# Two pre-activation attention layers on one core: sums held behind additions, weight differences on another engine, other banks for the last projection and the first statistics

## The chip, the cores and the metric

The kernel runs on one core of a Trainium2 chip. The metric is the device time of one execution in microseconds (us). Five engines work side by side, each through its own queue in order: PE (TensorE, matrix products), DVE (VectorE), ACT (ScalarE), POOL (GpSimd) and SP (SyncE), which here issues most of the transfers. Waits between engines go through semaphores. PE writes its results to PSUM, a small memory of eight banks[...].

## The reference, cut to what matters

Eight images of 32 x 32 tokens with 512 channels, in fp32, go through two layers. Each layer norms its input in 32 groups of channels, makes an attention over the 1024 tokens of an image and adds the result to its input.

```python
x = x + _L0_conv_ref(_gn(x), L0_conv_w_qkv, L0_conv_w_proj, L0_conv_b_proj)
x = x + _L1_conv_ref(_gn(x), L1_conv_Wq, L1_conv_Wk, L1_conv_Wv, L1_conv_Wo, L1_conv_pos_emb_w, L1_conv_pos_emb_h)
...
qkv = xt @ w_qkv                                    # layer 0: 16 heads of 32
attn = jax.nn.softmax(jnp.einsum('bhid,bhjd->bhij', q * SCALE, k), axis=-1)
out = jnp.einsum('bhij,bhjd->bhid', attn, v)        # then tokens x channels
out = out @ w_proj + b_proj
...
scores = attn_q @ k + pos.reshape(B, heads, L, L)   # layer 1: 4 heads of 128
attn = jax.nn.softmax(scores, axis=-1)
out = (attn @ v) @ Wo
```

## The kernel before, in words

**Layout.** Activations are kept transposed, channels on the 128 partitions and tokens along the row, in "blocks" of 128 x 4 x 1024 numbers. Every product of a block with a 512 x 512 weight is made in seven products of quarters instead of eight (`seven`, L397). Four sums of quarters of the activation go in as its "forms" (`forming`, L339, the additions at L360), and four differences of weight quarters (`add_up`, L140, the subtractions at L152) are made once and stored to DRAM; `stream` fetches quarters (`w_p`, `w_o`, `w_qkv` in the profile) on SP in the order of a list, `plan`. A block has two units `u`, and for each of them `seven` runs products into the banks `x`, `y` and `z`, in the order x0, y5, x1, y4, z6, y2, z3. After y5, DVE adds `a` = y + p1 (L411), after y4 `b` = y + p1 (L419); y4 cannot start before `a` is made from the same bank, and y2 not before `b`. ACT copies x to p1 and z to p7. The results leave through a sink: `Plain` for queries, keys and values, `Onto` for a projection with its residual, whose `gather` on POOL (L502) and `add` on DVE (L507, L509) put every part onto the block.

**Projections.** `WP` is the projection of layer 0, `WO` that of layer 1. `after_0` (L891) takes an attention output, makes its forms and runs WP onto the residual `x1T`, with the statistics of the next norm (L259) after each unit. `after_1` (L930) does the same with WO onto `x2T`; `put_out` (L941) transposes results on DVE (L947) and sends them off (L952). For the last image, `after_last` (L968) makes the two products of each unit that need no forms first (`two_first`, L437), then the forms, then the other five (`five_last`, L448).

**Norm.** `group_norm` (L265) is a chain of small DVE operations (`turned` L285 to `var` L296), one POOL operation (`rstd`, L300), and four DVE operations that scale the block (L304). `norm_1` (L905) runs it for the second layer; `second` (L910) begins with the forms of the normed block.

**First attention** (`attention_0`, L590). A step is four heads by 512 queries by 128 keys. `front` makes the scores in a PSUM tile `ps` of four banks, of which there is one (L603), and ACT takes the exponential into `e`, of which there are two (L611). `back` multiplies `e` with the values into the bank `acc` (L622) and DVE adds `e` to a running sum `es` (first two at L631, then L633). After eight steps `finish` sums `es` over the partitions on PE (L643), `normalise` (L560) turns that into reciprocals on DVE (L566 to L584), and POOL multiplies (L588).

**Order.** The loop at L1072 goes through images b = 0 to 8. While PE works on the first attention of image b, `side_by_side` (L995) puts between its steps, by their cost, everything of other images: WP of b-1, WO of b-2 woven with the norm of b-1 (`woven`, L983: from step `start` on, one step of the side work in every `gap`, at the `places` given), the projections and second attention of b-1, and the load, norm and projections of b+1. A scheduler then fixes the order on each engine; `tc.issue_after(x)` makes it place an instruction behind x on its engine. At b = 0 there is no earlier image: there the weights WP, WQ1, WK1, WV1 and WO are fetched and their differences made on POOL (`other_sums`, L1060), beside `before_0` of image 1. At b = 1, `other_keys` takes the place of WO.

**Start.** `load_first` (L811) brings image 0 in, turns it on PE (L830) into banks, of which the first half's four are one tile, copies them with ACT (L837), keeps PE busy with six matmuls whose result is not used (`idle`, L841), and takes the statistics from the copies.

Of the kernel before, what the change touches and what calls it, by code (L numbers as in the profile page):

```python
# [9 lines left out]
F32 = mybir.dt.float32  # L10
# [7 lines left out]
P = 128  # L18
# [9 lines left out]
def quick_path(  # L28
# [98 lines left out]
    class Matrix:  # L127
# [12 lines left out]
        def add_up(self, engines, store, keep=False):  # L140

            t = self.t
            whole = t[:, : CC // 2, :].rearrange("p a (b n) -> p (a b) n", n=NB)
            sums = t[:, CC // 2 :, :].rearrange("p a (b c n) -> p (a b) c n", c=HC, n=HN)
            b11, b12, b21, b22 = [quarter(whole, i) for i in (11, 12, 21, 22)]
            for i, (x, y) in enumerate(
                [(b12, b11), (b22, sums[:, 0]), (b22, b12), (b21, sums[:, 1])]
            ):

                engine = engines[i]  # L150
                with tc.issue_after(last_form[0].ins) if engine is nc.vector else nullcontext():
                    engine.tensor_tensor(sums[:, i], x, y, op=ALU.subtract)  # L152
            d = dram.tile([P, 4, HC, HN], F32, tag="sums", name=f"ws_{self.name}", bufs=8)
            store.dma_start(d, sums)
            self.t = d
            self.kept = (whole, sums) if keep else None
# [163 lines left out]

    added = [None]
# [75 lines left out]
    def seven(fs, u, rows, sink, name, hook=None):  # L397

        product = taken(fs, u, rows)
        x = bank(f"x_{name}")
        product(x, 0, True)
        p1 = snapshot("e1", f"p1_{name}")
        nc.scalar.copy(p1, x)
        yield HC
        y = bank(f"y_{name}")
        product(y, 5, True)
        a = snapshot("es1", f"a_{name}")  # L410
        begun[0] = nc.vector.tensor_add(a, y, p1)  # L411
        sink.early(p1, a)
        yield HC
        product(x, 1, False)
        sink.c11(x)
        yield HC
        product(y, 4, False)
        b = snapshot("es1", f"b_{name}")
        half_done[0] = nc.vector.tensor_add(b, y, p1)  # L419
        sink.middle(b)  # L420
        yield HC
        z = bank(f"z_{name}")
        product(z, 6, True)
        p7 = snapshot("e1", f"p7_{name}")
        nc.scalar.copy(p7, z)  # L425
        yield HC
        product(y, 2, False)
        sink.c12(y, p1)
        if hook is not None:
            hook()  # L430
        yield HC
        product(z, 3, False)
        sink.c21(z, a)
        sink.c22(b, p7)
        yield HC

    def two_first(fs, u, sink, name):  # L437

        product = taken(fs, u, False)
        x = bank(f"x_{name}")  # L440
        product(x, 0, True)
        p1 = snapshot("e1", f"p1_{name}")
        nc.scalar.copy(p1, x)
        product(x, 1, False)
        sink.c11(x)
        return p1

    def five_last(fs, u, sink, name, p1):  # L448
        product = taken(fs, u, False)
        y = bank(f"y_{name}")  # L450
        product(y, 5, True)
        a = snapshot("es1", f"a_{name}")
        nc.vector.tensor_add(a, y, p1)
        sink.early(p1, a)
        product(y, 4, False)
        b = snapshot("es1", f"b_{name}")
        nc.vector.tensor_add(b, y, p1)
        sink.middle(b)
        z = bank(f"z_{name}")
        product(z, 6, True)  # L460
        p7 = snapshot("e1", f"p7_{name}")
        nc.scalar.copy(p7, z)
        product(y, 2, False)
        sink.c12(y, p1)
        product(z, 3, False)
        sink.c21(z, a)
        sink.c22(b, p7)

# [121 lines left out]
    def attention_0(q, k, v, b, blocks=range(NT)):  # L590
# [23 lines left out]
        def back(m, h, j, e):  # L614
# [14 lines left out]
            if j == blocks[1]:  # L629
                state["esum"] = mem.tile([P, HB, NB], F32, tag="es0", name=f"es_{name}", bufs=1)  # L630
                nc.vector.tensor_add(state["esum"], state["first"], e)  # L631
            elif j != blocks[0]:
                nc.vector.tensor_add(state["esum"], state["esum"], e)  # L633
# [153 lines left out]
    def load(b, st):  # L787
# [21 lines left out]
        st["xn"] = yield from forming(x, f"xn0_{b}", behind=lambda: added[0])  # L809

    def load_first(st):  # L811
# [8 lines left out]
        xT = chunks(x)  # L820
        for h in range(NH):
# [13 lines left out]
            for cc in (0, 2, 1, 3):  # L835
                part = xT[cc][:, h * NB : (h + 1) * NB]
                nc.scalar.copy(part, banks[cc])  # L837

# [3 lines left out]
        for cc in (0, 2, 1, 3):  # L842
            statistics(st, xT, cc, "0_0")
# [47 lines left out]
    def after_0(b, st, hook=None):  # L891

        fs = st.pop("ao0") if "ao0" in st else forms(st["q0"], f"ao0_{b}", block(f"forms_{b}"))
        x = st["x1"] = block(f"x1T_{b}")
        xT = fetch(st["kept"], x)
        for u in range(2):
            bias = [bproj_sb[:, n * HC + u : n * HC + u + 1] for n in range(2)]
            stream.unit(WP, False, u)
            yield from seven(
                fs, u, False, Onto(halves(xT, u), bias), f"wp_{b}_{u}", hook if u else None  # L900
            )
            for n in range(2):
                statistics(st, xT, n * HC + u, f"1_{b}")

    def norm_1(b, st, after=None, behind=None):  # L905
        xT = chunks(st["x1"])
        st["kept"] = put_away(xT, f"1_{b}")
        yield from group_norm(st, xT, f"1_{b}", after, behind)

    def second(b, st):  # L910

        fs = forms(st.pop("x1"), f"xn1_{b}")
# [55 lines left out]
    def after_last(b, st):  # L968
# [4 lines left out]
        early = [x[:, :HC, :NB], x[:, HC:, :NB]]  # L973
        p1s = []
        for u in range(2):
            stream.unit(WO, False, u)
            p1s.append(two_first(early, u, sinks[u], f"wo_{b}_{u}"))
        fs = forms(x, f"ao1_{b}")
        for u in range(2):
            stream.unit(WO, False, u)  # L980
            five_last(fs, u, sinks[u], f"wo_{b}_{u}", p1s[u])
# [32 lines left out]

    def marked():
        in_place[0] = True
        return
        yield
# [14 lines left out]

    FIRST = units(WQ0) + units(WK0) + units(WV0, True)
    plan = [(m, m is WV0, u, ORDER) for u in range(2) for m in (WV0, WQ0, WK0)]
    for b in range(B + 1):
        if b >= 1:
            plan += units(WP)
# [8 lines left out]
    plan += [(WO, False, u, some) for some in (FIRST_TWO, LAST_FIVE) for u in range(2)]  # L1047
# [12 lines left out]
    def other_sums():  # L1060
        for m in (WP, WQ1, WK1, WV1, WO):
            m.fetch(nc.gpsimd)
            m.add_up([nc.gpsimd] * 4, nc.gpsimd)
# [8 lines left out]
    for b in range(B + 1):  # L1072
# [11 lines left out]
        if last is not None:  # L1084
            if past is not None:
                norm = norm_1(b - 1, last, after=lambda: half_done[0])
            else:
                norm = norm_1(b - 1, last, behind=lambda: begun[0])
            rest.append(after_0(b - 1, last, forms_past if past is not None else None))
            total += PRODUCT  # L1090
            if past is not None:
                rest.append(woven(later(after_1, b - 2, past), norm, 3, 3))
                total += PRODUCT
            else:
                rest.append(chain(woven(other_keys(b, here), norm, 0, 1), marked()))
# [19 lines left out]
        else:  # L1115
            rest.append(woven(rest_of_first(here), incoming, 0, 2))
            total += PRODUCT
        if coming is not None:

            before = later(before_0, b + 1, coming, forms_0 if last is not None else None)  # L1120
            rest.append(before if last is not None else woven(before, other_sums(), 2, 7))
# [500 lines left out]
```

## Time and profile before

| what | value |
|---|---|
| median of three runs | 3847.89 us (3846.76 to 3849.78) |
| profiled execution, its time | 3848.35 us |
| its span, first to last instruction | 3846.6 us |
| mean granted clock of PE | 0.998 |
| PE busy | 3789.4 us, 99% |
| DVE busy | 2555.1 us, 66% |
| ACT busy | 1760.2 us, 46% |
| POOL busy | 621.6 us, 16% |
| data moved | 234.72 MB, mean 61 GB/s |
| exponentials L611 | 512 of 1878 ns |
| sums L633 | 384 of 2330 ns |
| multiplications L588 on POOL | 128 of 1662 ns |

Lines of the page and of the trace give an engine, the line of the kernel, the operation with the names of its result and its operands, and times in microseconds. A timeline row has its start and its busy time first, then "xN" for how many instructions stand in it, and in brackets the idle time of the engine just before, with the instruction that ended it. In the list of waits, an entry such as "PE ps L603 <- ACT e L611" is the idle time of PE ahead of the scores, ended by an exponential: total, number, longest.

### The profile page before, as it was taken

The numbers are of one execution on the slowest core, as the hardware profiler recorded it, in microseconds if no ns is written. First come the engines' busy times: TensorE is split into PE (matmuls) and PEld (weight loads), VectorE is DVE, ScalarE is ACT, GpSimd is POOL, SyncE is SP. The second block draws the span as 40 slices with busy tenths as digits, with TensorE's granted clock in tenths as the row PEclk, the third lists the DMA queues.
The fourth block names the chain that finished last, engine by engine and source line by source line (L and its number), as shares of the span: only waits on it lengthen the run. The fifth ranks groups of instructions, "written<-read, shape, count | busy, mean of one in ns | idle before, by whom it ended". The sixth has DMA issues, their size and how long they took to land.

```text
span 3846.6 us, 79883 instructions
## 1 busy us (share of the span) xinstructions
PE 3789.4 (99%) x34478; PEld 1376.3 (36%) x34478; DVE 2555.1 (66%) x2966; ACT 1760.2 (46%) x1830; POOL 621.6 (16%) x398
## 2 busy tenths in 40 slices
PE   9999999999999999999999999999999999999998
PEld 4222244222443234432343323433234332334353
DVE  6777775686755866558665686656866568665544
ACT  3554544545444454444544445444454445553132
POOL 1342101121011211012101121111210112001201
PEclk9999999999999999999999999999999999999999
DMA  6122120142202322023120241103311023110321
GB/s 185 61 88 81 41 59 6 44 122 62 56 9 83 89 54 56 13 92 85 45 55 16 93 93 38 50 21 98 90 40 41 26 96 78 33 37 31 109 41 26
DMA packets 482983, 234.72 MB, mean 61 GB/s; under 512 B 269600, under 2 KB 461376, under 8 KB 481600
## 3 DMA queue, kind: packets, MB, share of 16 engines
q1 hardware_dynamic: 470992, 213.74, 20.5%
q0 software_dynamic: 2608, 13.70, 1.0%
q8 instruction: 273, 4.47, 0.5%
q10 hardware_dynamic: 9024, 2.10, 0.3%
q14 instruction: 86, 0.70, 0.1%
HBM read 170.72 MB, written 58.72 MB: 60 GB/s over the span
## 4 chain that ended last, share of the span: by engine, by line
PE 88%; DVE 7%; ACT 2%; issue 2%; DMA 0%; SPq 0%; POOL 0%; DVEq 0%; ACTq 0%; POOLq 0%
PE ps L603 12%; PE ps L718 11%; PE acc L730 11%; PE acc L622 11%; PE y_q L327 4%; PE y_v L327 4%; PE y_k L327 4%; PE ps L719 3%; PE x_q L327 3%; PE x_v L327 3%; PE z_k L327 3%; PE x_k L327 3%; PE z_q L327 3%; PE z_v L327 3%; DVE es L633 2%; ACT e L611 2%
## 5 line engine op out<-in xcount | busy, mean ns | idle before, releaser
L611 ACT ACTIVATE e<-ps 128x2048 f32<-128x2048 f32 x512 | 961.7, 1878 | 840.1 <-PE ps L603 630.0
L633 DVE TENSOR_TENSOR es<-es,e 128x2048 f32<-128x2048 f32 x384 | 894.8, 2330 | 403.7 <-ACT e L611 400.4
L603 PE MATMUL ps<-q,k 32*64 32x512 f32 x8192 | 579.1, 614 | 17.1 <-ACT e L611 17.1
L622 PE MATMUL acc<-e,v 128*32 128x512 f32 x4096 | 546.7, 605 | 0.0
L721 ACT ACTIVATE e<-ps 128x512 f32<-128x512 f32 x512 | 305.7, 597 | 507.1 <-PE ps L719 436.4
L718 PE MATMUL ps<-q,k 128*128 128x512 f32 x1024 | 525.0, 594 | 0.2 <-DVE posT L704 0.2
L730 PE MATMUL acc<-e,v 128*128 128x512 f32 x1024 | 522.0, 593 | 0.3 <-ACT e L721 0.3
L588 POOL TENSOR_TENSOR q<-q,su 128x512 f32<-128x512 f32 x128 | 212.7, 1662 | 1550.3 <-DVE su L584 1427.7
L741 DVE TENSOR_TENSOR es<-es,e 128x512 f32<-128x512 f32 x384 | 290.4, 756 | 251.0 <-ACT e L721 248.4
L719 PE MATMUL ps<-posT,sel 128*128 128x512 f32 x512 | 406.6, 794 | 0.0
L718 PEld LDWEIGHTS ps<-q,k 128*128 128x128 f32 x1024 | 192.5, 190 | 230.1 <-issue 218.5
L603 PEld LDWEIGHTS ps<-q,k 32*64 32x64 f32 x8192 | 120.6, 130 | 410.1 <-issue 223.5
L730 PEld LDWEIGHTS acc<-e,v 128*128 128x128 f32 x1024 | 193.1, 189 | 147.3 <-issue 92.6
L622 PEld LDWEIGHTS acc<-e,v 128*32 128x32 f32 x4096 | 81.3, 108 | 412.7 <-issue 366.1
L631 DVE TENSOR_TENSOR es<-e,e 128x2048 f32<-128x2048 f32 x64 | 171.6, 2681 | 32.8 <-ACT e L611 32.7
L568 DVE STREAM_TRANSPOSE tu<-su 128x512 f32<-128x512 f32 x128 | 90.5, 707 | 97.3 <-ACT su L566 95.7
L719 PEld LDWEIGHTS ps<-posT,sel 128*128 128x128 f32 x512 | 97.3, 190 | 122.5 <-issue 122.5
L566 ACT COPY su<-sums 128x512 f32<-128x512 f32 x128 | 74.9, 585 | 131.2 <-PE sums L643 81.5
L704 DVE TENSOR_TENSOR posT<-pp,posT 32x512 fp32r<-32x512 f32 x128 | 112.0, 875 | 31.9 <-ACT posT L699 30.6
L492 POOL TENSOR_TENSOR k<-b_k,p_k 128x512 f32<-128x512 f32 x32 | 52.0, 1624 | 483.4 <-ACT p_k L425 472.7
L699 ACT CAST posT<-pp 32x512 fp32r<-32x512 f32 x128 | 105.9, 827 | 45.8 <-PE pp L686 44.7
L492 POOL TENSOR_TENSOR v<-b_v,p_v 128x512 f32<-128x512 f32 x32 | 51.6, 1614 | 433.9 <-ACT p_v L425 433.9
(214 smaller groups left out, 4546.0 us busy)
## 6 DMA issues: line engine op xcount, KB each, us to landing
w_qkv<-ws_qkv SPq DMA_DIRECT2D x168, 128.0 KB, 2.5
d<-x0T SPq DMA_DIRECT2D x32, 512.0 KB, 3.0
x1T<-d SPq DMA_DIRECT2D x32, 512.0 KB, 5.9
d<-x1T SPq DMA_DIRECT2D x32, 512.0 KB, 3.6
x2T<-d SPq DMA_DIRECT2D x32, 512.0 KB, 6.1
w_qkv<-in_L_conv_w_qkv SPq DMA_DIRECT2D x126, 128.0 KB, 2.2
out<-ot SPq DMA_DIRECT2D x240, 64.0 KB, 2.0
xs<-in_x SPq DMA_DIRECT2D x224, 64.0 KB, 2.5
```

The lines of the kernel that those rows point to most:

```text
L327: ins = nc.tensor.matmul(out[columns, :], weights[:, columns], moving, start=start, stop=stop, skip_group_check=open_sum,)
L588: nc.gpsimd.tensor_tensor(dst, dst, su, op=ALU.mult)
L603: nc.tensor.matmul(ps[some, r, :], k[m][rows, j * P + 64 * i : j * P + 64 * i + 64], q[m][rows, h * NB : (h + 1) * NB], start=True, stop=True,
L611: nc.scalar.activation(e, ps, AF.Exp, scale=D0 ** -0.5)
L622: nc.tensor.matmul(acc[r * D0 : (r + 1) * D0, :], v[:, j, c0 : c0 + D0], e[:, r, :], start=(j == blocks[0]), stop=(j == blocks[-1]),)
L631: nc.vector.tensor_add(state["esum"], state["first"], e)
L633: nc.vector.tensor_add(state["esum"], state["esum"], e)
L718: nc.tensor.matmul(ps, k[h][:, keys], q[:, h, queries], start=True, stop=False)
L719: nc.tensor.matmul(ps, sel_flat[:, keys], posT[:, h, queries], start=False, stop=True)
L721: nc.scalar.activation(e, ps, AF.Exp, scale=1.0 / math.sqrt(D1))
L730: nc.tensor.matmul(acc, v[:, j, h * D1 : (h + 1) * D1], e, start=(j == 0), stop=(j == NT - 1),)
L741: added[0] = nc.vector.tensor_add(state["esum"], state["esum"], e)
```

## The change

It has five parts.

1. Around every norm of the second layer (WO woven with `norm_1` for b of 2 and more, and the first WP at b = 1), each sum `es` of the first attention is placed behind the last addition `a` or `b` (`reader`). The scalings of the norm (L304) and the forms of the normed block are placed behind sums (`summed`); the norm is taken up at steps 0, 2, 4, 8, 9 and 10 of every 14 instead of every third, with its forms behind it instead of at the head of `second`. At b = 1 the places are 0, 1, 2, 4, 5 and 6 of every 7.
2. At b = 0 the twenty weight differences of WP, WQ1, WK1, WV1 and WO are made on DVE instead of POOL, one by one, each behind a sum of the first attention. The load of image 1 is woven at every step instead of every second.
3. The first WP (image 0) is done in the way of the last WO: the two products of each unit that need no forms first, the forms between them, then the other five. For image 7 the statistics of the second unit are placed behind an addition `a`.
4. In the last WO, unit 1 takes its banks from the attention's PSUM: `x` in `acc`, `y` and `z` in a tile of four banks like `ps`. The forms are interleaved with the first products.
5. In `load_first`, the statistics (bn_stats) read the PSUM banks, each behind ACT's copy of the same bank, and are aggregated after the `idle` matmuls are issued.

The diff, cut to its core:

```diff
+        def adding(self, engines, store, behind, keep=False):
...
-                with tc.issue_after(last_form[0].ins) if engine is nc.vector else nullcontext():
+                with tc.issue_after(behind().ins) if engine is nc.vector else nullcontext():
                     engine.tensor_tensor(sums[:, i], x, y, op=ALU.subtract)
+                yield 0
...
+    reader = [None]
+    summed = [None]
+    beside_norm = [False]
...
-        begun[0] = nc.vector.tensor_add(a, y, p1)
+        reader[0] = begun[0] = nc.vector.tensor_add(a, y, p1)
...
-        half_done[0] = nc.vector.tensor_add(b, y, p1)
+        reader[0] = half_done[0] = nc.vector.tensor_add(b, y, p1)
...
+    def in_two_parts(x, m, sinks, name, room=None, done=lambda u: None, behind=None, banks=(bank, bank)):
+
+        early = [x[:, :HC, :NB], x[:, HC:, :NB]]
+        p1s, fs = [], []
+
+        def products():
+            for u in range(2):
+                stream.unit(m, False, u)
+                p1s.append((yield from two_first(early, u, sinks[u], f"{name}_{u}", banks[u])))
+
+        def sums():
+            fs.extend((yield from forming(x, name, room, behind)))
+
+        yield from woven(products(), sums(), 0, 1)
+        for u in range(2):
+            stream.unit(m, False, u)
+            yield from five_last(fs, u, sinks[u], f"{name}_{u}", p1s[u], banks[u])
+            done(u)
...
-                nc.vector.tensor_add(state["esum"], state["first"], e)
+                other = state["first"]
             elif j != blocks[0]:
-                nc.vector.tensor_add(state["esum"], state["esum"], e)
+                other = state["esum"]
+            if j != blocks[0]:
+
+                with tc.issue_after(reader[0].ins) if beside_norm[0] else nullcontext():
+                    summed[0] = nc.vector.tensor_add(state["esum"], other, e)
...
+        looks = small.tile([P, CC, NH, 6], F32, tag="looks", name="looks")
...
                 nc.scalar.copy(part, banks[cc])
+                nc.vector.bn_stats(looks[:, cc, h, :], banks[cc])
...
-        for cc in (0, 2, 1, 3):
-            statistics(st, xT, cc, "0_0")
+        for cc in range(CC):
+            nc.vector.bn_aggr(
+                st["mv"][:, : 2 * CC].rearrange("p (s c) -> p c s", c=CC)[:, cc, :],
+                looks[:, cc].rearrange("p h s -> p (h s)"),
+            )
...
+        if "ao0" not in st:
+            yield from in_two_parts(
+                st["q0"], WP, sinks, f"wp_{b}", block(f"forms_{b}"), done, lambda: summed[0]
+            )
+            return
...
+    def sums_1(b, st):
+
+        st["xn1"] = yield from forming(st.pop("x1"), f"xn1_{b}", behind=lambda: summed[0])
...
+        idle = [psum.tile([P, NB], F32, tag="acc", name="wo_acc", bufs=1)]
+        scores = psum.tile([P, HB, NB], F32, tag="ps", name="wo_ps", bufs=1)
+        idle += [scores[:, r, :] for r in range(HB)]
+        run(in_two_parts(x, WO, sinks, f"wo_{b}", banks=(bank, lambda name: idle.pop(0))))
...
-            m.add_up([nc.gpsimd] * 4, nc.gpsimd)
+            yield from m.adding([nc.vector] * 4, nc.gpsimd, lambda: summed[0])
...
-                norm = norm_1(b - 1, last, after=lambda: half_done[0])
+                norm = norm_1(
+                    b - 1, last, after=lambda: half_done[0], behind=lambda: summed[0]
+                )
...
+            norm = chain(norm, later(sums_1, b - 1, last))
...
-                rest.append(woven(later(after_1, b - 2, past), norm, 3, 3))
+                rest.append(with_norm(woven(later(after_1, b - 2, past), norm, 3, 14, (0, 2, 4, 8, 9, 10))))
...
-                rest.append(chain(woven(other_keys(b, here), norm, 0, 1), marked()))
+                rest.append(chain(woven(other_keys(b, here), norm, 0, 7, (0, 1, 2, 4, 5, 6)), marked()))
```

## The prediction

> **What bounds the kernel now.** I read the page's busy times first, then the chain that ended last, then the list of what TensorE (PE) waited for, and last the timeline around each of those waits. The page says that PE is busy for 3789.4 us of a span of 3846.6 us, and the chain runs through PE for 88% of it:
>
> ```profile
> PE 3789.4 (99%) x34478; PEld 1376.3 (36%) x34478; DVE 2555.1 (66%) x2966; ACT 1760.2 (46%) x1830; POOL 621.6 (16%) x398
> ...
> PE 88%; DVE 7%; ACT 2%; issue 2%; DMA 0%; SPq 0%; POOL 0%; DVEq 0%; ACTq 0%; POOLq 0%
> ```
>
> The change keeps PE's matmuls, so only the other 57.2 us (3846.6 - 3789.4) can be won. PE's waits (total, times, longest) say where they lie:
>
> ```profile
> PE ps L603 <- ACT e L611: 17.1, 16, 2.9
> PE y_wo L327 <- DVE a_wo L411: 9.1, 6, 1.8
> ...
> PE x_v L327 <- issue: 3.5, 1, 3.5
> PE sums L643 <- DVE es L633: 3.1, 2, 1.8
> PE y_wp L327 <- DVE forms L360: 2.5, 1, 2.5
> ```
>
> In five images, 471 us apart, the same two waits return. The timeline of one (start, duration, engine, line, operation; in brackets the idle time before and its releaser):
>
> ```profile
> 1314.33 2.98 DVE L304 TENSOR_SCALAR x1T<-x1T,back,rstd 128x1024 f32<-128x1024 f32 x4 [1.20 <-POOL rstd L300]
> ...
> 1317.23 2.28 DVE L633 TENSOR_TENSOR es<-es,e 128x2048 f32<-128x2048 f32 x1
> ...
> 1319.60 1.88 ACT L611 ACTIVATE e<-ps 128x2048 f32<-128x2048 f32 x1 [5.25 <-DVE es L633]
> ...
> 1321.54 1.12 PE L603 MATMUL ps<-q,k 32*64 32x512 f32 x16 [0.98 <-ACT e L611]
> ```
>
> Four scalings of the norm stand ahead of a sum `es`; the exponential needs the buffer that this sum frees; PE needs the exponential to empty its scores. The second wait, 9 us on: two sums hold back `a_wo`, which frees the bank of the next product.
>
> ```profile
> 1325.24 4.64 DVE L633 TENSOR_TENSOR es<-es,e 128x2048 f32<-128x2048 f32 x2
> ...
> 1329.80 0.68 DVE L411 TENSOR_TENSOR a_wo<-y_wo,p_wo 128x512 f32<-128x512 f32 x1
> ...
> 1330.54 1.92 PE L327 MATMUL y_wo<-f_ao,w_o 128*32 128x512 f32 x16 [1.42 <-DVE a_wo L411]
> ```
>
> In the first attention GpSimd (POOL) makes the weight differences while DVE makes the sums:
>
> ```profile
> 156.08 9.38 DVE L633 TENSOR_TENSOR es<-es,e 128x2048 f32<-128x2048 f32 x2
> ...
> 156.23 3.76 POOL L152 TENSOR_TENSOR prep_q<-prep_q 128x512 f32<-128x512 f32 x3
> ...
> 165.60 1.07 PE L643 MATMUL sums<-es,ones 128*32 128x512 f32 x8 [1.82 <-DVE es L633]
> ```
>
> Two sums took 9.38 us; elsewhere one takes 2.28.
>
> **What the Trainium skill says.** "SBUF — State Buffer", Who interferes with whom: a DVE instruction with two SBUF inputs contends with a GpSimd instruction that reads SBUF. The trace agrees: 4.69 us for a sum beside L152 against 2.28 alone, and 2.4 to 3.3 us for a POOL subtraction against 1.27. "PSUM — Partial Sum Buffer", PSUM bank collisions: two engines may not touch one bank and quadrant at once, reads by ScalarE and VectorE included, so such reads must be ordered. Parts 4 and 5 put several banks into one tile, and in the changed instruction list they are ordered for the whole tile; no row of before has it. "TensorE: Matmul & The Clock Gate", Part 1: an idle array falls to half its clock and needs some 3.4 us of work to recover. The first `x_v` product agrees: 32 records in 3.46 us, where the next takes about 1.73.
>
> **Part 1, the norms.** In the changed order each sum stands behind the last a or b addition, and the scalings are split in pairs with a sum ahead. Working it with before's times: sum 3 of the row starts at about 1313.0, inside the 1.20 us in which DVE waited for `rstd`, and ends at 1315.3 instead of 1319.5. Its exponential then waits only for its scores, which end at about 1317.85: 1.75 us earlier than 1319.60, more than the 0.98 us of PE's wait. `a_wo` of the second unit moves ahead of its sum and ends at about 1327.3; PE reaches that product at 1329.1 less the 0.98 already won, so the 1.42 goes too. What is late next: `a_wo` of the first unit ahead of sum 1 makes exponential 2 end 0.65 later, 0.3 us before PE's scores need it, and sum 2 has 1.6 us. Nothing else on DVE is behind by more. So 0.98 + 1.42 = 2.4 us an image, 12.0 for five (bounds 5 and 13.5: one wait left, or the slow matmuls after each wait won too). The sixth norm (waits of 1.19 at 3186.99 and 1.31 at 3214.35) is reordered alike: I take 1.5 of 2.5. In the last one `a_wo` is moved ahead of the statistics, and its 1.62 us wait goes: 1.6. The second image's scalings keep their order, so the 1.85 us wait at 376.34 stays.
>
> **Part 2, twenty subtractions to DVE.** 20 x 0.62 us (L152 on DVE at 26.52: five in 3.09) is 12.4 us of DVE, set in gaps of 0.9 to 1.9 us in front of its sums; in exchange each sum beside them falls from about 4.6 to 2.3 us. The last sum then no longer keeps PE waiting at 165.60 (1.82), and the 16 score matmuls after it, slow by 1.82 - 1.11 = 0.71, run at full clock: 2.5. At 137.7 there is a wait of 2.9, but `k`'s addition stands next and would make the following product wait some 1.8, so 0.5 there; 1.0 for five smaller ones. Sum 4.0 (bounds 1 and 7). The first subtraction of each matrix now waits on DVE for its fetch, with sums behind it. Fetches landed 5.7 to 8.0 us after issue on POOL's queue; the first is issued at 135.8 and read at about 156, the others are issued two sums or more ahead, so I count nothing; a fetch late by 3 us would cost that once. The stores wait for DVE on POOL's queue, with a multiplication (L588) behind; POOL was idle for 10 to 20 us there.
>
> **Part 3, first WP.** The 3.5 us of `x` products of the second unit move ahead of `y_wp`, whose forms were late by 2.50 us; the 1.04 us wait ahead of it and the slow product (2.94 against 1.92) go with it: 4.5 (bounds 2 and 5.5). The fetch of `x1T` on SP moves ahead of a weight fetch; it took 5.9 us to land and is needed later than that. POOL's gather now stands before the L588 that the forms need; if `x1T` were late, the forms would be too.
>
> **Part 4, last WO.** `y`, then `z` and `y` of unit 1 lie in one tile. In the changed list the second `y` waits for `a_wo`, `z` for `b_wo`, the next `y` for `z`'s copy, the last `z` for an addition of `y`. Each is 0.59 to 0.69 us and about 0.25 of handing over, four in a row, 3.6 us; before, where a product stood between, these cost 1.1. So +2.5 (bounds 0 and 3.6).
>
> **Part 5, first statistics.** `bn_stats` (0.64) and ACT's copy (0.51) now alternate on the four banks of one tile, and statistics end at about 16.9 instead of 15.6: xn +1.25. The `idle` matmuls (5.32) wait for the last look and run until 22 to 23.5 us, ahead of `x_v`, which then runs warm (1.7 less). But `y_v` now stands ahead of the second `x_v` and needs the second form (25.6), and the following `y_v` needs `a_v`, behind five L152 on DVE (31.8; before 30.27). `b_v` stands behind five more (35.5; before 33.27), and less of the next product is done ahead. I get the first `y_q` ending at 42.3 against 39.1: +3.2 (bounds 0 and 5).
>
> **Sum.** -12.0 - 1.5 - 1.6 - 4.0 - 4.5 + 2.5 + 3.2 = -17.9 us. The profiled execution took 3848.35 us (span 3846.60 and 1.75 around it), 0.46 above the median of 3847.89. So 3830.4 there, and 3830.0 as a median. A difference of 0.2% (7.7 us) is about what a measurement can tell from none.
>
> **Rivals.**
> - Everything is won (0.12): 2.7 in each norm with the slow matmuls, 2.6 and 1.8 in the two others with theirs, 5.5 and 6 in parts 3 and 2, and start and end cost 1 each: -13.5 - 4.4 - 11.5 + 2 = -27.4, 3820.5. For it: the waits stand in the trace. Against it: the tile-wide orders.
> - The waits partly shift (0.18): only 0.98 goes in each norm (4.9), 1.6 in the last, 2.5 and 2 in parts 3 and 2, while start and end cost 4.5 and 3.5: -3.0, 3845. For it: only 0.3 us of slack behind the first `a_wo`.
> - Slower (0.10): the additions that now stand ahead of every sum make all exponentials late. An addition costs 0.65; what goes beyond the 0.3 us of slack, 0.35, falls on each of about seven held sums in seven places: +17.2. With no gain in the norms and the rest at -1.6 - 4.0 - 4.5 + 5.7 = -4.4, this is +12.8, 3861. It decides from the point where PE's score matmuls wait in every round beside a norm. Against it: in before PE has one wait there in nine rounds, and sum 2 has 1.6 us.
> - That the change doesn't do what it says is excluded by the order of instructions.
>
> **How the numbers follow.** My forecast holds 0.60, with its own range 3823 to 3838. Faster by over 0.2% means below 3840.2: 0.60 + 0.12 + 0.05 of the shifted case = 0.77. Within 0.2%: 0.13. Slower: 0.10. The range 3818 to 3845 leaves out the slower case, half of the shifted one at most, and the extreme of the best.
>
> **What would show it.** In the profile after: no wait of a `y_wo` product for `a_wo` (L411 of before) and none of the scores for the exponential in the five norms, the L304 rows split x2; sums near 2.3 us at 141 to 271; no wait of `y_wp` for forms; the first `y_q` some 3 us later; four waits of 0.9 in the last 12 us. I am wrong if PE's waits for exponentials grow in number, or if start and end lose more than 10 us together.

## The result, and the profile after

The changed kernel takes 3858.48 us (median of 13 runs, 3855.73 to 3861.51), the kernel before 3847.74 us (13 runs). The ratio is 1.0026, with a 95% interval of 1.0019 to 1.0033: slower by 10.7 us. The forecast was 3830.0, its range 3818 to 3845. The profiled execution has a span of 3857.9 us. Its busy times, and what PE waited for (total, times, longest):

```profile
PE 3793.1 (98%) x34478; PEld 1370.3 (36%) x34478; DVE 2573.5 (67%) x2986; ACT 1762.0 (46%) x1830; POOL 613.4 (16%) x378
```

```profile
PE ps L637 <- ACT e L645: 25.6, 22, 4.2
PE idle L883 <- DVE looks L879: 5.5, 1, 5.5
...
PE y_wp L335 <- DVE a_wp L463: 2.6, 2, 1.8
PE y_q L335 <- DVE a_q L419: 2.1, 5, 0.4
...
PE y_k L335 <- DVE b_k L427: 1.5, 1, 1.5
...
PE wo_ps L335 <- DVE x2T L541: 0.8, 1, 0.8
PE wo_ps L335 <- DVE b_wo L468: 0.8, 1, 0.8
PE wo_ps L335 <- ACT p_wo L474: 0.8, 1, 0.8
```

The six long waits of `y_wo` are gone, and so is the one of `y_wp` for its forms. The exponential now keeps PE waiting 22 times instead of 16, and for up to 4.2 us: a growing number of these waits was one of the two signs of being wrong that the prediction named. To see where the time went, both traces can be laid side by side: the first attention's score matmuls are 512 groups of 16, 64 an image, in one order in both kernels. In the first image they are called groups below, in the others rounds, counted from 0 within an image. The start of each group after, less its start before, is the delay so far; where it jumps, something was lost or won.

| stretch | delay at its end | change, us | forecast |
|---|---|---|---|
| to the first scores (part 5) | 2.71 | +2.7 | +3.2 |
| first image, groups 0 to 47 (part 2) | 1.38 | -1.3 | -4.0 |
| first image, groups 48 to 51 (part 2) | 8.75 | +7.4 | 0 |
| first WP (part 3) | 7.22 | -1.5 | -4.5 |
| five norms (part 1) | 3.65 | -3.6 | -12.0 |
| seventh image's norm (part 1) | 8.20 | +4.6 | -1.5 |
| last norm, second attention | 8.02 | -0.2 | -1.6 |
| last WO (part 4) | 11.24 | +3.2 | +2.5 |

This compares one execution of each kernel. In two rows a part of the loss is slow matmuls after a long wait: 2.7 of the +7.4 and 2.8 of the +4.6; the latter did not follow in every execution, as the last section shows.

The start: the chain of small norm operations begins 1.1 us later, and PE's `idle` matmuls, which came after a wait, ran for 8.26 us instead of 5.32.

```profile
15.79 0.70 DVE L879 BATCH_NORM_STATS2 looks<-turned 128x6 f32<-128x512 f32 x1 [0.27 <-ACT x0T L878]
...
16.64 8.26 PE L883 MATMUL idle<-x_rows,ident 128*128 128x512 f32 x12 [5.51 <-DVE looks L879]
```

In groups 0 to 47 the two waits that the prediction wanted to shorten did shrink, by 1.1 us at group 19 and, with slow matmuls after it, by 3.7 us up to group 26. But `y_k` now waits for its `b_k`, which stands behind two forms of image 1 and a sum; this cost 2.6 us.

```profile
133.24 1.48 PE L335 MATMUL y_k<-f_xn,prep_qkv 128*32 128x512 f32 x9 [1.52 <-DVE b_k L427]
```

The wait of 4.2 us in the first image: ACT's copy into the values `v` of image 1 waits for the store of WV1's weight differences, whose block `v` takes over. The last subtraction (L155) stands behind a sum, the store follows it, and the exponential stands behind the copy in ACT's queue.

```profile
254.11 0.69 DVE L155 TENSOR_TENSOR prep_v<-prep_v 128x512 f32<-128x512 f32 x1
...
255.09 0.58 POOL L158 DMA_DIRECT2D ws_v<-prep_v  x1 [17.67 <-DVE prep_v L155]
...
260.11 0.59 ACT L516 COPY v<-x_v 128x512 f32<-128x512 f32 x1 [5.40 <-DMA ws_v<-prep_v]
260.59 1.88 ACT L645 ACTIVATE e<-ps 128x2048 f32<-128x2048 f32 x1
...
262.52 2.01 PE L637 MATMUL ps<-q,k 32*64 32x512 f32 x16 [4.18 <-ACT e L645]
```

One of the five norms, the same as was shown of before: the scalings are split, `a_wo` of the second unit stands ahead of its sum, and neither of the two waits is there.

```profile
1319.66 2.28 DVE L671 TENSOR_TENSOR es<-es,e 128x2048 f32<-128x2048 f32 x1
...
1322.86 1.53 DVE L308 TENSOR_SCALAR x1T<-x1T,back,rstd 128x1024 f32<-128x1024 f32 x2 [0.91 <-POOL rstd L304]
...
1327.52 1.11 PE L637 MATMUL ps<-q,k 32*64 32x512 f32 x16
...
1333.74 0.68 DVE L419 TENSOR_TENSOR a_wo<-y_wo,p_wo 128x512 f32<-128x512 f32 x1
...
1334.91 1.90 PE L335 MATMUL y_wo<-f_ao,w_o 128*32 128x512 f32 x16
```

They were worth 1.05 and 1.63 us in the comparison of the traces. But three others have come: 0.5 us behind the first `a_wo` (round 11), and 0.9 and 0.6 us in the comparison where the next projection begins (rounds 19 and 20).

```profile
1314.52 1.12 PE L637 MATMUL ps<-q,k 32*64 32x512 f32 x16 [0.44 <-ACT e L645]
...
1353.23 1.12 PE L637 MATMUL ps<-q,k 32*64 32x512 f32 x16 [0.86 <-ACT e L645]
...
1357.49 1.92 PE L335 MATMUL y_q<-f_xn,w_q 128*32 128x512 f32 x16 [0.42 <-DVE a_q L419]
```

In the seventh image the first sum of a block stands behind `a_wo`, and that behind the normalisation; the exponential waits for the sum:

```profile
3222.24 0.71 DVE L618 STREAM_TRANSPOSE su<-rc 128x512 f32<-128x512 f32 x1
...
3222.87 0.65 DVE L419 TENSOR_TENSOR a_wo<-y_wo,p_wo 128x512 f32<-128x512 f32 x1
...
3223.45 3.07 DVE L671 TENSOR_TENSOR es<-e,e 128x2048 f32<-128x2048 f32 x1
...
3226.61 1.88 ACT L645 ACTIVATE e<-ps 128x2048 f32<-128x2048 f32 x1 [5.59 <-DVE es L671]
...
3228.54 2.01 PE L637 MATMUL ps<-q,k 32*64 32x512 f32 x16 [3.04 <-ACT e L645]
```

### The profile page after: what moved, and what is told of

It reads as the page before. It is cut to its first block, busy times and chain, and to the rows that moved or that the text cites. A ratio compares the mean times of both kernels' runs of the same rounds, so it can differ in the third digit from the quotient of the medians.

```text
span 3857.9 us, 79906 instructions
## 1 busy us (share of the span) xinstructions
PE 3793.1 (98%) x34478; PEld 1370.3 (36%) x34478; DVE 2573.5 (67%) x2986; ACT 1762.0 (46%) x1830; POOL 613.4 (16%) x378
## 4 chain that ended last, share of the span: by engine, by line
PE 87%; DVE 8%; ACT 2%; issue 1%; DMA 1%; POOL 0%; DVEq 0%; SPq 0%; ACTq 0%; POOLq 0%
PE ps L637 12%; PE ps L756 11%; PE acc L768 11%; PE acc L656 11%; PE y_k L335 4%; PE y_v L335 4%; PE y_q L335 4%; DVE es L671 3%; PE ps L757 3%; PE z_k L335 3%; PE z_q L335 3%; PE x_v L335 3%; PE x_k L335 3%; PE z_v L335 3%; PE x_q L335 3%; PE y_wp L335 2%
## 5 line engine op out<-in xcount | busy, mean ns | idle before, releaser
L622 POOL TENSOR_TENSOR q<-q,su 128x512 f32<-128x512 f32 x128 | 200.1, 1563 | 1521.0 <-DVE su L618 1386.3
```

Of the source, the lines that this page charges most:

```text
L622: nc.gpsimd.tensor_tensor(dst, dst, su, op=ALU.mult)
```

## The experiments

My theory after the traces: the loss is a sum of separate waits, each with its own cause, and what the norms gain is mostly given back. The rival: the sums held behind additions make everything on DVE late, and the separate waits are its symptoms. Each version below was timed in turn with the kernel before, whose medians were 3847.35 to 3847.93 us. Within a version the executions spread by 2.7 to 7.4 us, so differences of about 1 us between two versions can't be told from none.

| version | executions | median, us | ratio to before, 95% |
|---|---|---|---|
| changed, part 5 undone | 10 | 3858.11 | 1.0025 (1.0015 to 1.0034) |
| changed, part 4's banks undone | 17 | 3854.85 | 1.0020 (1.0013 to 1.0027) |
| changed, part 2 undone | 13 | 3851.19 | 1.0010 (1.0002 to 1.0018) |
| changed, sums free in the seventh image | 19 | 3854.20 | 1.0019 (1.0012 to 1.0026) |
| changed, differences begun earlier | 20 | 3853.01 | 1.0014 (1.0007 to 1.0021) |
| A: the four undone together | 21 | 3841.83 | 0.9985 (0.9978 to 0.9991) |
| A, held behind the second a only | 21 | 3841.92 | 0.9984 (0.9978 to 0.9991) |
| that, first WP in one part | 21 | 3843.60 | 0.9987 (0.9981 to 0.9994) |
| B: A, held behind a and b of the second unit only | 21 | 3842.19 | 0.9985 (0.9978 to 0.9991) |
| B, third form later | 17 | 3841.72 | 0.9983 (0.9976 to 0.9991) |
| A with part 5 | 13 | 3846.12 | 0.9996 (0.9987 to 1.0004) |
| B with part 2 begun earlier | 21 | 3844.32 | 0.9990 (0.9984 to 0.9997) |
| B, five images' output transposes left out | 5 | 3832.88 | 0.9958 (0.9944 to 0.9972) |
| B, third form on GpSimd | 13 | 3850.66 | 1.0006 (0.9998 to 1.0014) |

**One part undone at a time.** First the statistics of image 0:

```diff
-                nc.vector.bn_stats(looks[:, cc, h, :], banks[cc])
...
+        for cc in (0, 2, 1, 3):
+            statistics(st, xT, cc, "0_0")
```

> The changed kernel with part 5 undone: the first statistics read the copies in SBUF again. Theory (each part carries its own loss, and a loss stays until the end): the first scores start at about 60.0 us as in before instead of 62.7, nothing later takes that back, so 2.7 us less than the changed kernel's 3858.5: about 3855.8. Rival (waits on transfers and weights later in the first image take up a late start): no change, 3858.5.

Measured: 0.4 us less. The first scores do start 2.73 us earlier; in the profiled execution this was lost again in the first WP (1.6 us) and at the norm after it (1.7 us), where PE's matmuls ran slowly after waits of 1.76 and 1.85 us that are the same in both kernels. The median stands nearer to the rival, but the ten executions lie between 3854.11 and 3860.34 us, and that doesn't exclude the theory's 2.7 us. The last projection's banks:

```diff
-        run(in_two_parts(x, WO, sinks, f"wo_{b}", banks=(bank, lambda name: idle.pop(0))))
+        run(in_two_parts(x, WO, sinks, f"wo_{b}"))
```

> The changed kernel with the last projection's unit 1 in the ordinary banks again. Theory: the four waits of 0.70 to 0.82 us in the last 12 us, one behind the other, are due to the one tile for y and z; about 3.3 us less than 3858.5, so 3855.2. Rival (y4 directly after y5 is the cause, the tile is not): only 0.5 to 1 us less, 3857.8.

Measured: 3.6 us less; the one tile is the cause. In the changed kernel these waits follow each other:

```profile
3837.43 1.92 PE L335 MATMUL wo_ps<-f_wo,w_o 128*32 128x512 f32 x16 [0.70 <-DVE a_wo L463]
...
3840.16 1.92 PE L335 MATMUL wo_ps<-q,w_o 128*32 128x512 f32 x16 [0.81 <-DVE b_wo L468]
...
3842.84 1.92 PE L335 MATMUL wo_ps<-f_wo,w_o 128*32 128x512 f32 x16 [0.75 <-ACT p_wo L474]
...
3845.57 1.92 PE L335 MATMUL wo_ps<-q,w_o 128*32 128x512 f32 x16 [0.81 <-DVE x2T L541]
```

The weight differences on GpSimd again, woven as before:

```diff
-            yield from m.adding([nc.vector] * 4, nc.gpsimd, lambda: summed[0])
+            m.add_up([nc.gpsimd] * 4, nc.gpsimd)
...
-            rest.append(woven(rest_of_first(here), incoming, 0, 1))
+            rest.append(woven(rest_of_first(here), incoming, 0, 2))
...
-            rest.append(before if last is not None else woven(before, other_sums(), 2, 1))
+            rest.append(before if last is not None else woven(before, other_sums(), 2, 7))
```

> The changed kernel with part 2 undone: the weight differences on GpSimd again, and the weaving of before around them. Theory: the wait of 4.2 us at 258 us (a copy into v on ACT waits for the store of the differences of WV1, whose last subtraction stands behind a late sum) and the slow matmuls after it go, the first image's balance of +6.0 us returns to about 0: 3852.5. Rival (the sums beside GpSimd, 4.6 us instead of 2.3, cost as much as the new wait): 3857 to 3860.

Measured: 7.3 us less, the theory. The sums free beside the seventh image's norm:

```diff
-        beside_norm[0] = True
+        beside_norm[0] = held
...
-                rest.append(with_norm(woven(later(after_1, b - 2, past), norm, 3, 14, (0, 2, 4, 8, 9, 10))))
+                rest.append(with_norm(woven(later(after_1, b - 2, past), norm, 3, 14, (0, 2, 4, 8, 9, 10)), b < B - 1))
```

> The changed kernel, but beside the norm of the seventh image (b = 7) the sums of the first attention are not placed behind the additions. Theory: the wait of 3.0 us at 3225 us and the slow matmuls after it come from the sum of the first two exponentials standing behind an addition that itself stands behind the normalisation; they go, 5.6 us less: 3852.9. Rival (the scalings and forms in their new places are what delays DVE there): within 1 us of 3858.5.

Measured: 4.3 us less. The wait is 1.42 us instead of 3.04, and in its profiled execution no slow matmuls follow; so holding is the larger part. The 1.2 us by which the wait still exceeds before's 0.20 stay, presumably with the new places of scalings and forms. Then the cause of the wait for the store, with part 2 left in place:

```diff
-            rest.append(before if last is not None else woven(before, other_sums(), 2, 1))
+            rest.append(before if last is not None else woven(before, other_sums(), 0, 1))
```

> The changed kernel, with the weight differences on DVE as in the change, but the weaving of these steps begins two steps earlier (at step 0 of the projections of image 1 instead of step 2). Theory (the wait of 4.2 us at 258 us is for the landing of the store of WV1's differences, whose block the values of image 1 take over): the last of these subtractions comes two sums earlier, some 7 us, the store has landed before the copy into v, the wait and the slow matmuls after it go: 5.5 to 7 us less than 3858.5, about 3852. Rival (the 20 subtractions load DVE too much in these rounds, wherever they stand): no change, 3857 to 3860.

Measured: 5.5 us less, the theory. The last subtraction of WV1 is at 246.33 us instead of 254.11, the copy waits 1.09 us for the store instead of 5.40, and PE doesn't wait there:

```profile
246.33 0.68 DVE L155 TENSOR_TENSOR prep_v<-prep_v 128x512 f32<-128x512 f32 x1
247.31 0.58 POOL L158 DMA_DIRECT2D ws_v<-prep_v  x1 [7.34 <-DVE prep_v L155]
...
251.66 0.59 ACT L516 COPY v<-x_v 128x512 f32<-128x512 f32 x1 [1.09 <-DMA ws_v<-prep_v]
```

**All four together.** The edits above (without the last) in one kernel, version A:

> The changed kernel with the four losses found so far taken out together: weight differences on GpSimd, the last projection's banks and the first statistics as before, and the sums free beside the norm of the seventh image. What is left is the holding of sums in five norms and the first WP in two parts. Theory (the losses add up; left is -0.64 us in each of five norms and -1.5 us in the first WP): 3847.5 - 4.7 = 3842.8. Rival (they overlap, since part of each is taken back later): 3847 to 3850.

Measured: 3841.83, so 16.7 us less than the changed kernel, where the single steps sum to 0.4 + 3.6 + 7.3 + 4.3 = 15.6. So the losses do not overlap, as the theory said; that the sum comes so close is partly luck, since part 5 counts 0.4 here and 4.3 in A (below). The rival of this section, that held sums make everything late, falls: in A most sums beside the norms are still held.

**What the norms gain, and why so little.** Version A, held behind one addition only:

```diff
-        reader[0] = begun[0] = nc.vector.tensor_add(a, y, p1)
+        begun[0] = nc.vector.tensor_add(a, y, p1)
+        if name.endswith("_1"):
+            reader[0] = begun[0]
...
-        reader[0] = half_done[0] = nc.vector.tensor_add(b, y, p1)
+        half_done[0] = nc.vector.tensor_add(b, y, p1)
```

> As the kernel before it in this list (the four losses taken out), and sums stand behind the a addition of the second unit only, no longer behind the a and b of the first or the b of the second. Theory: of the norm's gains (1.05 and 1.63 us) both stay, since the first comes from the split scalings and the second from that one a; of its new waits the 0.5 us at the first a and the 1.5 us at the start of the following projection (forms behind a sum behind b) go: 2.0 us less in each of five norms, 10 us together, 3833. Rival (the late sums at the following projection come from the forms standing behind sums, not from b): only 0.5 us a norm, 3840.

Measured: no gain (3841.92), less than even the rival expected. The 0.5 us at the first `a` went, but `b` of the second unit now comes late by 0.85; 0.55 is then won at round 19. In sum -0.2 us a norm. The first WP in one part again (`in_two_parts` replaced by `forms` and `seven`):

> As the kernel before it in this list, and the first WP is done in one part again, as in the kernel before the change. Theory (two parts save the 3.6 us of waits and 1.6 us of slow matmuls there, and cost 0.84, 0.82 and 1.77 us of new waits for a, since the last five products have no product between y5 and y4): 1.5 us more than that kernel, 3834.5. Rival (the new waits cost as much as the old, slow matmuls included): equal within 0.7 us.

Measured: 1.7 us more. That is nearer to the theory, though the executions of the two versions overlap widely; in the comparison of the two traces it is 1.9 us after the first WP. So part 3 is worth some 1.5 to 2 us, not 4.5. In the changed kernel, `y4` follows `y5` at once and waits for `a`:

```profile
344.51 1.92 PE L335 MATMUL y_wp<-forms,w_p 128*32 128x512 f32 x16 [0.82 <-DVE a_wp L463]
...
362.20 1.92 PE L335 MATMUL y_wp<-forms,w_p 128*32 128x512 f32 x16 [1.77 <-DVE a_wp L463]
```

Version B sets `reader` at the a and at the b of the second unit:

> As the version with the four losses taken out (3841.8), and sums stand behind the a and the b addition of the second unit, no longer behind those of the first. Theory: the new wait of 0.5 us at the first a goes, and the 0.85 us that came when b of the second unit was left behind a sum does not come: 0.5 us less in each of five norms, 2.5 us together, 3839.3. Rival (the wait comes from elsewhere in that round): 3841.8.

Measured: no gain (3842.19), the rival's number but not its reason: the 0.5 us at round 11 went in every norm, and 0.4 to 0.5 came back at round 19. And B with one place fewer for the norm's side work, so that the third form comes behind the first sum:

```diff
-    woven(later(after_1, b - 2, past), norm, 3, 14, (0, 2, 4, 8, 9, 10))
+    woven(later(after_1, b - 2, past), norm, 3, 14, (0, 2, 4, 8, 9))
```

> As the kernel before it in this list, and the norm's side work is taken up at one place fewer of the 14, so that the third form of the normed block comes behind the first sum of the next block of queries instead of ahead of its normalisation. Theory (the 0.9 us wait at round 19 of each norm is DVE's queue: three forms, two additions and a transpose ahead of the normalisation and the sum that frees the exponential's buffer): the sum comes 1.2 us earlier and the wait goes, 0.9 us in each of five norms, 4.5 us less, 3834.8. Rival (the third form is late now in its turn, and the products wait for it or for a): no gain, 3839.

Measured: no gain (3841.72), the rival. 1.1 us went at round 19, and 1.1 came back one round later, as a wait for `a_q`, which now stands behind the late form:

```profile
1347.80 1.93 PE L335 MATMUL y_q<-f_xn,w_q 128*32 128x512 f32 x16 [1.55 <-DVE a_q L419]
```

Three more orders, one sum. So I asked whether DVE is simply full there. In 26 us of the kernel before, from 1328, it is busy for 25.3, and in 26 us of B, from 1321, for 25.8 (columns: length, then busy time and records of PE, PEld, DVE, ACT and POOL, PE's clock, DMA). First the kernel before, then B:

```profile
1328.00:1354.00 26.00, 24.58 (x264) 6.27 (x256) 25.32 (x26) 12.10 (x10) 6.65 (x3) 1.00 0.57 102
```

```profile
1321.00:1347.00 26.00, 24.75 (x260) 6.18 (x256) 25.83 (x26) 11.52 (x9) 9.69 (x3) 1.00 0.50 90
```

B with work left out, the transposes of five images' outputs:

```diff
-            with tc.issue_after(added[0].ins) if late else nullcontext():
-                nc.vector.transpose(ot, xT[m][:, h * NB : (h + 1) * NB])
+            if b > 4:
+                with tc.issue_after(added[0].ins) if late else nullcontext():
+                    nc.vector.transpose(ot, xT[m][:, h * NB : (h + 1) * NB])
+            else:
+                ot = xT[m][:, h * NB : (h + 1) * NB]
```

> The version whose sums stand behind a and b of the second unit only (3842.2), with work left out: for images 0 to 4, whose results are written beside the five norms, the transposes of the results on DVE are not made, and the blocks are sent as they are, so that these outputs are in the wrong order. 8 x 0.7 = 5.6 us of DVE less in each norm, the same transfers. Theory (in rounds 8 to 20 of a norm DVE has work for nearly all of the time, so its queue, not the order, sets PE's waits there): the two waits that are left, 1.3 and 0.6 us, go, and the order changes nothing more: 1.9 us in each of five norms, 9.5 us less, 3832.7. Rival (a chain of latencies, from the last scores through sums, normalisation and first sum, sets them, and DVE is idle often enough): less than 2 us in all, 3841.

Measured: 9.3 us less (3832.88, five executions), the theory to 0.2 us. In the 52 us of this norm PE waited for 1.25 us in B and now never does, and DVE is busy for 47.84 us instead of 49.13. First B, then with the work left out:

```profile
1295.00:1347.00 52.00, 50.75 (x524) 12.92 (x520) 49.13 (x63) 24.54 (x18) 22.98 (x10) 1.00 0.44 100
```

```profile
1294.00:1346.00 52.00, 52.00 (x540) 13.44 (x536) 47.84 (x57) 24.65 (x20) 22.97 (x10) 1.00 0.50 109
```

This shows that DVE's work in the stretch makes the waits. It doesn't show that no order could help: in the kernel before, DVE is busy for only 14.05 of the 26 us that follow (1354 to 1380), and an order that moves transposes out there was not tried.

And B with the third form on another engine, nothing left out:

```diff
-            (nc.vector.tensor_sub, a21, a11, a21),
+            ((third or nc.vector).tensor_sub, a21, a11, a21),
```

> The same version with the third form of the normed block, beside the norms only, made on GpSimd instead of DVE; nothing is left out. 1.2 us of DVE less, one GpSimd operation of 128 x 1024 more, some 2.5 us alone. Theory (DVE's work sets the waits there): about 1 us less in each of five norms, 5 us, 3837. Rival (sums and additions beside GpSimd grow by as much as DVE is spared, as sums beside the weight differences grew from 2.28 to 4.69 us): 3842 or up to 3 us more.

Measured: 8.5 us more (3850.66). In the trace it is about 1.1 us in each of the five norms and 0.8 in the sixth; most of the rest are slow matmuls after two waits. That is the rival's mechanism and more than its size: while GpSimd made the form, an addition on DVE that takes 0.68 us took 2.87.

```profile
1335.64 3.42 POOL L368 TENSOR_TENSOR x1T<-x1T 128x1024 f32<-128x1024 f32 x1 [1.16 <-DVE f_xn L372]
...
1336.74 2.87 DVE L549 TENSOR_TENSOR x2T<-p_wo,x2T 128x512 f32<-128x512 f32 x1
...
1339.53 0.68 DVE L549 TENSOR_TENSOR x2T<-y_wo,x2T 128x512 f32<-128x512 f32 x1
```

**Parts 5 and 2 once more,** in kernels with fewer other waits. A with the first statistics from PSUM:

> The version with the four losses taken out (3841.8), with part 5, the first statistics from PSUM, put back. Theory (part 5 delays the first scores by 2.7 us, and where the first image has no other new wait nothing takes this back): 3844.5. Rival (the later waits of the first image absorb it, as undoing part 5 alone seemed to show): 3841.8 within 0.7.

Measured: 4.3 us more, somewhat above the theory's 2.7, where undoing the same part in the changed kernel gave 0.4. The first scores come 2.2 us later here and 2.7 there. How much of it stays until the end differs between the two traces with the waits and slow matmuls after it, and I can't say by which of them. B with the differences on DVE, begun two steps earlier:

> As the first kernel of this list, with the weight differences on DVE in the way of part 2, begun two steps earlier so that the store is in time. Theory (without the wait for the store, part 2 is worth little: the ledger of the changed kernel shows 1.3 us less up to the 43rd round of the first image): 1.3 us less than the first kernel of this list, 3838.0. Rival (the sums without GpSimd beside them are worth the 4.0 us that the prediction took): 3835.3.

Measured: 2.1 us more than B. Theory and rival both fall, and with them my price for part 2: even without the wait for the store, part 2 gains nothing. In its profiled execution, `y_k` waits for its `b`, as in the changed kernel (2.6 us later than in B), and this is won back by group 59; 1.7 us of slow matmuls at 375 are not. What the 2.1 us are is not settled.

## Why the prediction was wrong, step by step

- **Part 1, "Nothing else on DVE is behind by more. So 0.98 + 1.42 = 2.4 us an image".** Both waits went as worked out (1.05 and 1.63 in the comparison). The step that failed is the sentence before the sum: I looked for the next late thing only as far as the second wait, round 16, and took freed waits as won. DVE is busy for 25.3 of 26 us there, so the four orders that were run only moved the wait along its queue, among rounds 11, 17, 19 and 20; with less work it went. The term of 12.0 was 3.6. And "makes exponential 2 end 0.65 later" was too little: with `a_wo` in between, POOL's multiplication starts ahead of the sum instead of behind it, and the sum takes 3.07 us instead of 2.25 in these norms too (at 1309.40, before at 1302.32). So 0.65 + 0.82 = 1.5 us later, past the slack, and PE waits 0.44 to 0.5.
- **The sixth norm, "is reordered alike".** Not so: there `a` falls behind the normalisation, and the first sum of the next block behind `a`. -1.5 was +4.6 in the comparison, 2.8 of it slow matmuls that do not follow this wait in every execution; holding cost 4.3 us by the version with free sums.
- **The last norm, "its 1.62 us wait goes".** It went, but two of 0.47 and 0.69 us came 8 and 12 us further on (3591.71 and 3596.04): DVE makes its scalings and additions there at nearly the same times as before, and PE, now earlier, waits for them. -1.6 was -0.2.
- **Part 2, "so I count nothing" for the fetches and stores.** I asked who waits for the fetch and what stands behind the store on POOL's queue, but not which buffer the store keeps: the values of image 1 take over its block, and an exponential stands behind their copy. This is the largest term, +7.4: 4.2 us of wait and the slow matmuls after it.
- **Part 2, "each sum beside them falls from about 4.6 to 2.3 us".** The gain was mis-sized too: 1.3 by the comparison, none by the timed version, against 4.0. The 4.6 was half of a row of two sums in 9.38 us. The chain that ended last has the two apart (start, duration); the first ran beside three subtractions, and its end and the second beside an addition of POOL (L492) that stays there:

```profile
156.08 6.09 DVE es L633
162.26 3.20 DVE es L633
```

  Fifteen sums of the kernel before overlap a subtraction. The other fourteen took 2.3 to 3.2 us, and all fifteen together 7.4 us more than at 2.28 each, while the twenty subtractions brought DVE 12.4 us by the prediction's own count. So DVE lost by the exchange. (The 2.4 us of "2.4 to 3.3 us for a POOL subtraction" is that addition too; the subtractions beside sums took 1.3 to 3.3.) What came late through it, or through the denser weaving of image 1, was not separated; `b_k` above is one such addition.
- **Part 3.** The forms no longer keep PE waiting, as said. I priced the missing product between y5 and y4 in the tail, and forgot it in the same function here: 0.82 and 1.77 us of waits for `a`. 4.5 was 1.5 in the comparison and 1.7 timed.
- **Part 4** was right in mechanism; four waits of 0.70 to 0.81 us. +2.5 was +3.2 in the comparison and 3.6 timed.
- **Part 5** was right for the first scores: +2.7 against +3.2. But the `idle` matmuls, counted with 5.32 us, took 8.26. What of the delay lasts is between 0.4 and 4.3 us.
- **The slower rival** named 3861, near the measured time, but by luck: its mechanism was exponentials late in every round beside a norm, and in the five norms they were late in two rounds, 11 and 19, by 0.4 to 0.9 us. It is the store, the tile, the start and one image that made the kernel slower.

The Trainium skill, "SBUF — State Buffer", Who interferes with whom, says that a DVE instruction with two SBUF inputs contends with a GpSimd instruction that reads SBUF, as I quoted; the 2.87 us above show it again. I drew the gain from it for part 2, too large, and not the loss: a sum that starts behind a GpSimd instruction pays it.

## What to carry to other kernels

Before a wait is counted as won by a new order, add up the busy time of the engine that causes it over the stretch up to where it is next idle: if it is full, another order within the stretch may only move the wait, as the four here did, and less work in it helps, as leaving the transposes out did. For a step that is moved, ask not only what it waits for but which buffer it holds until it is done, and what is queued behind the next user of that buffer. And where buffers are put into one tile, count a hand-over for each of its users in turn.

The best versions here, A and those near it, take the first WP in two parts and the split norm and leave the rest: 3841.7 to 3842.2 us, 0.15% to 0.17% faster than before and not told apart among themselves.

## What the runs showed of the hardware

Which of DVE and GpSimd is slowed depended on which started first, with few exceptions. In the version with the seventh image's sums free, the sum starts 0.22 us ahead of the multiplication: 2.25 us for the sum, 3.17 for GpSimd. In the changed kernel GpSimd starts 0.36 us ahead, and it is 1.28 and 3.07. First the free version, then the changed kernel:

```profile
3223.74 2.25 DVE L671 TENSOR_TENSOR es<-e,e 128x2048 f32<-128x2048 f32 x1
3223.96 3.17 POOL L622 TENSOR_TENSOR q<-q,su 128x512 f32<-128x512 f32 x1 [3.73 <-DVE su L618]
```

```profile
3223.09 1.28 POOL L622 TENSOR_TENSOR q<-q,su 128x512 f32<-128x512 f32 x1 [4.37 <-DVE su L618]
3223.45 3.07 DVE L671 TENSOR_TENSOR es<-e,e 128x2048 f32<-128x2048 f32 x1
```

In the sixteen traces of this case, 1156 sums that overlap a single GpSimd operation of 128 x 512 start ahead of it, and 1151 of them take less than 2.4 us; 633 start behind it, and 586 of them take longer. With several operations in a row it can be otherwise: the sum of 6.09 us above starts 0.15 us ahead of three subtractions, which keep their 1.3 us each.

A long wait of PE costs more than itself in some executions. The same wait in the seventh image, 3.04 us in the changed kernel and 3.05 in the version with part 4's banks undone, was followed in the first by 16 score records in 2.01 us (above) and in the second by the usual 1.12:

```profile
3229.99 1.12 PE L637 MATMUL ps<-q,k 32*64 32x512 f32 x16 [3.05 <-ACT e L645]
```

The slow stretch cost 2.8 us in the comparison of these two traces. The clock granted to PE was 0.50 in the 4 us after the wait in the first and 1.00 in the second. Five traces have this wait; in three of them the clock fell to 0.50. The wait of 4.2 us in the first image stands in four traces, and slow score matmuls followed in all four. The Trainium skill, "TensorE: Matmul & The Clock Gate", Part 1, says that an array that has been idle for a window of some 3.4 us drops to half its clock until it has worked for as long, and that the window runs freely; the half clock and the chance agree with that. But a wait of 1.76 us was followed by slow matmuls too (part 5 undone, granted clock 0.57 from 360 to 364 us), so here shorter waits were enough. The slow stretches also fit the wider spread of the changed kernel's runs, 5.8 us against 3.2; that this is the cause of the spread was not tried.
